# Two layers of windowed attention and experts on one core: layer 1 softmax shifts for two query blocks by one product, and the layer 0 output bias added on VectorE

## The chip, the cores and the metric

The kernel runs on one core of a Trainium2 chip. The metric is the device time of one execution in microseconds; lower is better. The engines are TensorE (PE; its weight loads are listed as PEld), VectorE (DVE), ScalarE (ACT), GpSimd (POOL) and SyncE (SP, which issues most of the DMAs). Every engine works through its own list of instructions in a fixed order, and semaphores make it wait for others.

## The reference, cut to what matters

The input x is 4 batches of 512 tokens with 128 features, in fp32. Two layers follow each other, and each is x + s * silu(f), where s is an attention and f a mixture of 8 experts, both on a normalised x.

```python
x = L0_attn_x
xn = _layernorm(x)
s = _L0_attn_ref(xn, ...)          # 16 heads of 8, keys of the last 64 tokens, scaled logits, then:
                                   #   out @ w_o + b_o
g = _silu(_L0_ffn_ref(xn, ...))    # one expert of 8 for each token: gelu(x @ w1 + b1) @ w2 + b2
x = x + s * g
xn = _layernorm(x)
s = _L1_attn_ref(xn, ...)          # layer norm, q, k, v, windowed attention, projection,
                                   #   then a dense gelu block of 512
g = _silu(_L1_ffn_ref(xn, ...))    # again one expert of 8 for each token, with relu
x = x + s * g
```

The windowed attention of layer 1 takes blocks of 64 queries with their own 64 keys, at steps of 32 tokens, and blends the overlapping halves:

```python
for i in range(0, S, w2):          # w2 = 32
    start, end = max(0, i - w4), min(S, i + window_size - w4)
    attn = softmax(einsum('bqd,bkd->bqk', qw, kw), axis=-1)
    wo = einsum('bqk,bkd->bqd', attn, vw)
    ...                            # blended with what the block before left
```

## The kernel before, in words

The kernel is one function, `two_layers`. Its work is written as 32 generators ("threads"), one for each stage: `project0`, `scores_q`, `fitness0`, `masked0`, `scores_k`, `values0`, `outs0` and `combine0` are the attention of layer 0; `prepare1`, `project1`, `queries1`, `scores_k1`, `values1`, `outs1`, `contexts1` and `feed1` that of layer 1; `route`, `moe_load`, `moe_load_2`, `moe_x`, `moe_h`, `moe_y` and `gates` the experts, once for each layer.

`run` (L357) interleaves the threads with a planner. Each step says what it needs, and after its instructions `spent(cost, steps, events)` books its cost on TensorE (times a pace of 1.12 after the first 70 us, and 1.8 before) and the steps that follow on the other engines. The planner takes the step that can start first, with the ranks listed at L1482 and after to break ties. The order on TensorE is the order in which steps are taken. Where the planner sees TensorE idle, `awake` (L113) puts in bf16 matmuls of ones into the bank that is about to be used, one for each 0.3 us of 0.8 times the gap. `copied` (L342) gives a copy out of PSUM to the engine, ScalarE or VectorE, that the books show free first.

The steps that the change touches:

- `outs0` (L1127). For each of the four batches it transposes the attention result into `attT`, and the output product `s` gets four groups of two fp32 matmuls: the bias row `o0` by a row of ones (1 row by 128), then `attT` by `wo0_sb`. If the gate of that batch is near, `combine` (L1160) multiplies straight from PSUM (L1163) and adds x (L1164); otherwise `copied` moves the sum to the tile `s0`, and `combine0` does that later. The new x is normalised in `prepare1` (L437 to L449 and `centred`, L428), which is what layer 1 and the router of the second expert pass start from.
- `queries1` (L1236). For each of 16 tiles (4 batches by 4 tiles of 128 tokens): products of scores `s1`, with queries on partitions, for two query blocks `w` of 64 in each of two parities `par`; their negated maxima `mx` (L1288); `split` (L465) writes each maximum as a sum of three bf16 terms into 12 of the 32 columns that a group of four heads has in `shb`; two bf16 transposes on TensorE (`tr_sh`) put these rows on partitions; ScalarE copies them to `shd` (L1296, 256 columns); four VectorE multiplications by `smask` (L1299) spread them over the four heads of a group into `sh4`.
- `scores_k1` (L1303). The products of scores again, now with keys on partitions (tile `e`): in each parity 8 fp32 matmuls of 32 rows by 64 columns, and then 8 bf16 matmuls that add the shifts, of 12 rows by 64 columns, since each query block needs its own columns of `sh4`. ScalarE takes the exponential of both halves (L1331). `values1` then multiplies by v.

The constants are made in a set-up that VectorE works through between the first layer norms: `jmask` (L840), `smask` (L842), `blend` (L826 to L828). L766 is the offset of a layer norm of layer 0, which ScalarE waits for. `feed1` (L1411) is layer 1's projection and dense block; its product `fy` for the last batch is the last on TensorE.

Of the kernel before, what the change touches and what calls it, by code (L numbers as in the profile page):

```python
# [16 lines left out]
P = 128  # L17
# [40 lines left out]
def two_layers(  # L58
# [145 lines left out]
    def prepared(name, n, shape, dtype=F32, one=None):  # L204
        got = []
        for i in range(n):
            t = const.tile(shape, dtype, tag=f"{name}{i}", name=f"{name}{i}")
            nc.gpsimd.memset(t, 0.0)
            if one:
                nc.gpsimd.memset(one(t), 1.0)  # L210
            got.append(t)
        return got
# [697 lines left out]
    for i in range(2):  # L910
        nc.gpsimd.tensor_copy(
            ves[i][:, 0 : H * VC].rearrange("p (h d) -> p h d", d=VC)[:, :, HD], valid[:, i : i + 1].to_broadcast([P, H])
        )
    shbs1 = prepared("shb1_", 2, [P, 2, G, 32], BF16)
    later.close()


# [209 lines left out]
    def outs0():  # L1127
        for i in range(NTILE):
            b, t = divmod(i, NT)
            yield "M", [("ov0", i)]  # L1130
            if t == 0:
                att0[b] = att_p.tile([P, NT, D], F32, tag="att0", name=f"att_{b}", bufs=1)
            tp = transposed(ovs0.pop(i), f"o0_{b}_{t}").rearrange("p (j g e) -> p j g e", j=J, g=G)
            rec = small.tile([P, J, G], F32, tag="rec0", name=f"rec0_{b}_{t}")
            nc.vector.reciprocal(rec, tp[:, :, :, HD])
            nc.vector.tensor_tensor(
                att0[b][:, t, :].rearrange("p (g j d) -> p j g d", g=G, j=J), tp[:, :, :, 0:HD],
                rec[:, :, :, None].to_broadcast([P, J, G, HD]), ALU.mult,
            )
            spent(0.5, [("D", 0.5)], [("o0", i)])  # L1140
            if t < NT - 1:
                continue
            yield "M", [("o0", i)]
            attT = tok.tile([P, T], F32, tag="attT", name=f"attT_{b}", bufs=1)
            copied(attT, transposed(att0[b], f"att_{b}"), 0.5, [("attT", b)])
            yield "M", [("attT", b)] + ([("x1", b - 1)] if b - 1 in s0 else [])
            ps = bank(f"s0_{b}")
            for u in range(NT):
                o = ps[:, u * D : (u + 1) * D]
                mm(o, ones[0:1, :], row("o0")[0:1], start=True, stop=False)  # L1150
                mm(o, attT[:, u * P : (u + 1) * P], wo0_sb, start=False, stop=True)
            ps = ps.rearrange("p (t d) -> p t d", t=NT)
            if at.get(("gate", 0, b), 1e9) < now["T"] + 3.0:
                combine(b, ps)
                spent(1.5, [("D", 0.7), ("D", 0.7)], [("so", b), ("x1", b), ("acc", 0, b)])
            else:
                s0[b] = tok.tile([P, NT, D], F32, tag="s0", name=f"s0_{b}", bufs=1)
                copied(s0[b], ps, 1.5, [("so", b)])

    def combine(b, s):  # L1160

# [40 lines left out]
    def project1():  # L1202

        for b in range(B):
            yield "-", [("xn1", b), ("s1", (b - 1) * NT - 1)]
            xh = tok.tile([P, NT, D], F32, tag="ln", name=f"xh_{b}", bufs=3)
            with behind_steps("A", at["xn1", b]):
# [28 lines left out]
    def queries1():  # L1236


        for i in range(NTILE):
# [49 lines left out]
                    mx.rearrange("p a g j -> p g a j")[:, 2 * gg : 2 * gg + 2], ps[gg], AX.X, ALU.max, negate=True,  # L1289
                )  # L1290
            shb = shbs1[i % 2]
            split(shb, mx, f"1_{b}_{t}")
            spent(1.15, [("D", 2.45), ("D", 1.0)], [("s1", i), ("shb", i)], scores=1)
            yield "M", [("shb", i), ("e1", i - 2)]
            shd = att_p.tile([P, 2 * P], BF16, tag="shd1", name=f"shd1_{b}_{t}")
            nc.scalar.copy(shd, transposed16(shb.rearrange("p a g r -> p a (g r)"), 2, f"sh1_{b}_{t}"))  # L1296
            sh4 = att_p.tile([P, 2, J, P], BF16, tag="sh4_1", name=f"sh4_1_{b}_{t}")
            for j in range(J):
                nc.vector.tensor_scalar_mul(sh4[:, :, j], shd.rearrange("p (a f) -> p a f", a=2), smask[:, j : j + 1])  # L1299
            asked1[i] = q4, sh4, v  # L1300
            spent(0.13, [("A", 0.4), ("D", 1.2)], [("sh1", i)])

    def scores_k1():  # L1303
        for i in range(NTILE):
# [9 lines left out]
            for par in range(2):  # L1314
                for w in range(2):
                    o = par * 2 * HALO + w * KB
                    for g in range(G):
                        r = slice(32 * g, 32 * g + 32)
                        mm(
                            ps[g // 2][w * KB : (w + 1) * KB, g % 2, par], kd[r, t * P + o : t * P + o + KB],  # L1320
                            q4[r, :, o : o + KB], start=True, stop=False,
                        )
                for w in range(2):
                    for g in range(G):
                        r = slice(32 * g, 32 * g + NS * J)
                        mm(
                            ps[g // 2][w * KB : (w + 1) * KB, g % 2, par], ones16[r, 0:KB],
                            sh4[r, par, :, w * KB : (w + 1) * KB], start=False, stop=True,
                        )
            for gg in range(2):  # L1330
                nc.scalar.activation(pt[:, 2 * gg : 2 * gg + 2], ps[gg], AF.Exp, scale=SCALE)  # L1331
            pts1[i] = pt, v
            spent(1.45, [("Ae", 1.03), ("Ae", 1.03)], [("e1", i)], scores=2)

    def values1():
        for i in range(NTILE):
# [223 lines left out]
```

## Time and profile before

| | |
|---|---|
| median of 3 runs | 489.83 us (489.01 to 495.69) |
| the profiled execution | 503.98 us |
| its span | 502.3 us |
| mean granted clock of TensorE | 0.941 |
| TensorE busy | 430.1 us, 86% |
| weight loads | 299.9 us, 60% |
| VectorE busy | 339.5 us, 68% |
| ScalarE busy | 261.2 us, 52% |
| GpSimd busy | 179.7 us, 36% |

A line of a group reads: line, engine, operation, the tile written and those read, the shapes, the number of records; then busy time in us and the mean of one record in ns; then the idle time ahead of them and what ended it. An fp32 matmul shows as two records. The line of a matmul or transpose is that of its helper (L83, L88), so they are told apart by tiles; the profile leaves out numbers in names, so that `s` is both the scores and the output sum, and `e` is the second product of scores in both layers. Records of matmuls overlap: their busy time is not the time that TensorE is held, which shows in the distance from one start to the next. A timeline line reads: start in us, time that the merged records cover in us, engine, line, operation, tiles, shapes, number of records, and idle time ahead in brackets. A windows line reads: stretch, its length, busy us (and records) of PE, PEld, DVE, ACT and POOL, the granted clock, the DMA share and GB/s.

### The profile page before, as it was taken

Reading aid. Unit: us, or ns where it says so; the run is one execution under the profiler, and the core shown is the slowest. Engines: PE = TensorE matmul, PEld = TensorE weight load, DVE = VectorE, ACT = ScalarE, POOL = GpSimd, SP = SyncE. Lnnn points to the kernel's source line nnn. Section 1 sums busy time; section 2 is a strip of 40 time slices with the busy share of each in tenths; the row PEclk is TensorE's granted clock in tenths of the full one; section 3 lists DMA queues with packets and bytes.
Section 4 is the critical chain, followed back from the end, with each engine's and each line's share of the span. In section 5 each row is a group of like instructions: output and inputs, shape, how many; then the busy total and the mean of one; then the engine's idle time right before and its main releaser. Section 6 shows DMA issues by size and latency. Waiting matters only on the chain.

```text
span 502.3 us, 14768 instructions
## 1 busy us (share of the span) xinstructions
PE 430.1 (86%) x5690; PEld 299.9 (60%) x5690; DVE 339.5 (68%) x1011; ACT 261.2 (52%) x512; POOL 179.7 (36%) x251
## 2 busy tenths in 40 slices
PE   5876887999999657799999899779889887899885
PEld 2642554676665432355565575557769676788763
DVE  6899987552855987887774658964556535765565
ACT  1422655696676644574436637445476333536522
POOL 5842444455422232342310304045342337532311
PEclk8787799999999996899999979999999998989999
DMA  5405444756253010100000000141452764532032
GB/s 168 129 1 140 120 139 117 220 135 181 43 129 97 16 54 23 42 23 2 18 8 3 1 1 23 35 126 29 124 169 65 170 167 124 163 96 68 18 103 65
DMA packets 61894, 42.12 MB, mean 84 GB/s; under 512 B 11328, under 2 KB 54208, under 8 KB 61824
## 3 DMA queue, kind: packets, MB, share of 16 engines
q1 hardware_dynamic: 58464, 34.85, 25.3%
q0 software_dynamic: 2944, 6.04, 4.4%
q8 instruction: 45, 0.74, 0.6%
q10 hardware_dynamic: 416, 0.29, 0.2%
q14 instruction: 25, 0.20, 0.1%
HBM read 34.99 MB, written 6.16 MB: 82 GB/s over the span
## 4 chain that ended last, share of the span: by engine, by line
PE 57%; DVE 25%; issue 8%; ACT 7%; POOL 2%; DMA 1%; SPq 0%; DVEq 0%; ACTq 0%; POOLq 0%
PE e L83 11%; PE s L83 8%; PE h L83 7%; PE y L83 6%; PE ov L83 5%; DVE mx L1009 3%; PE fy L83 3%; PE f L83 2%; ACT th L1017 2%; DVE mx L1288 2%; PE pr L83 2%; PE v L83 2%; PE qkv L83 1%; PE o L88 1%; DVE sm L1009 1%
## 5 line engine op out<-in xcount | busy, mean ns | idle before, releaser
L666 POOL DMA_INDIRECT yt<-yb,put_at x46 | 46.2, 1005 | 105.3 <-DVE yb L664 21.0
L609 POOL DMA_INDIRECT xb<-xd,tokens_at x46 | 45.3, 985 | 56.6 <-DVE tokens_at L586 16.9
L83 PE MATMUL h<-xbT,wb 128*128 128x128 f32 x368 | 51.4, 290 | 3.0 <-ACT xbT L344 1.3
L83 PE MATMUL y<-wb,hb 128*128 128x128 f32 x368 | 49.3, 282 | 3.3 <-ACT hb L696 2.5
L83 PEld LDWEIGHTS h<-xbT,wb 128*128 128x128 f32 x368 | 46.3, 201 | 9.7 <-issue 4.1
L83 PE MATMUL e<-q,kd 32*64 32x256 f32 (+1 forms) x864 | 48.4, 444 | 1.5 <-issue 0.9
L83 PEld LDWEIGHTS y<-wb,hb 128*128 128x128 f32 x368 | 45.3, 195 | 7.1 <-ACT hb L696 2.9
L1288 DVE TENSOR_REDUCE mx<-s 128x16 f32<-128x1024 f32 x32 | 37.6, 1218 | 7.8 <-PE s L83 5.9
L1331 ACT ACTIVATE pt<-e 128x1024 f32<-128x1024 f32 x32 | 31.0, 1021 | 20.5 <-PE e L83 17.4
L1017 ACT ACTIVATE th<-s 128x768 f32<-128x768 f32 x32 | 26.0, 814 | 29.8 <-DVE mx L1009 29.2
L83 PE MATMUL s<-k,qd 32*32 32x384 f32 (+1 forms) x1024 | 37.4, 473 | 2.6 <-ACT pt L1331 2.3
L83 PEld LDWEIGHTS <-ones 12*64 12x64 bf16 (+2 forms) x434 | 21.4, 107 | 26.5 <-issue 18.6
L344 ACT COPY osb<-ov 128x512 f32<-128x512 f32 x32 | 18.1, 587 | 35.1 <-PE ov L83 26.4
L1106 ACT ACTIVATE pt<-e 128x1024 f32<-128x1024 f32 x32 | 31.0, 1021 | 10.1 <-PE e L83 10.1
L1009 DVE TENSOR_REDUCE mx<-s 128x8 f32<-128x768 f32 x32 | 29.3, 950 | 8.0 <-PE s L83 6.6
L696 ACT ACTIVATE hb<-h,bb 128x128 f32<-128x128 f32 x92 | 26.6, 381 | 14.3 <-PE h L83 10.8
L83 PE MATMUL ov<-pt,va 64*32 64x128 f32 (+1 forms) x896 | 30.6, 290 | 3.2 <-issue 2.8
L1009 DVE TENSOR_REDUCE sm<-th 128x8 f32<-128x768 f32 x32 | 30.1, 946 | 1.1 <-ACT th L1017 0.7
L1249 POOL TENSOR_TENSOR q<-qd,jmask 128x640 f32<-128x640 f32 x16 | 19.9, 1257 | 29.6 <-PE e L83 27.4
L83 PEld LDWEIGHTS e<-q,kd 32*64 32x64 f32 x864 | 20.6, 136 | 14.6 <-issue 9.7
L344 DVE COPY osb<-ov 128x512 f32<-128x512 f32 x16 | 11.0, 688 | 23.8 <-PE ov L83 17.1
L83 PEld LDWEIGHTS ov<-pt,va 64*32 64x32 f32 (+1 forms) x896 | 17.6, 106 | 10.7 <-issue 6.0
(287 smaller groups left out, 922.4 us busy)
## 6 DMA issues: line engine op xcount, KB each, us to landing
wb<-in_w SPq DMA_DIRECT2D x92, 256.0 KB
bb<-in_b SPq DMA_DIRECT2D x46, 64.0 KB
acc<-yt SPq DMA_DIRECT2D x8, 256.0 KB
xd<-ln_a SPq DMA_DIRECT2D x4, 256.0 KB
xd<-xr SPq DMA_DIRECT2D x4, 256.0 KB
out<-acc SPq DMA_DIRECT2D x8, 128.0 KB
x<-in_x SPq DMA_DIRECT2D x3, 256.0 KB
bb<-in_cols SPq DMA_DIRECT2D x46, 2.0 KB
```

The lines of the kernel that those rows point to most:

```text
L83: ins = nc.tensor.matmul(*args, **kw)
L88: ins = nc.tensor.transpose(dst, src, ident)
L344: (nc.scalar.copy if e == "A" else nc.vector.tensor_copy)(dst, src)
L609: nc.gpsimd.indirect_dma_start(out=xb, out_offset=None, in_=xd, in_offset=bass.IndirectOffsetOnAxis(ap=tokens_at[:, k : k + 1], axis=0),)
L666: nc.gpsimd.indirect_dma_start(out=yt, out_offset=bass.IndirectOffsetOnAxis(ap=routed[n][0][:, k : k + 1], axis=0), in_=y, in_offset=None,)
L696: nc.scalar.activation(h[:, c, :], src[:, c * P : (c + 1) * P], AF.Gelu, bias=bias[:, c : c + 1])
L1009: nc.vector.tensor_reduce(dst[:, t, 8 * gg : 8 * gg + 8].rearrange("p (u j) -> p u j", u=2), src.rearrange("p u (j f) -> p u j f", j=J), A ...
L1017: nc.scalar.activation(th, ps[gg], AF.Tanh, scale=0.5 * SCALE)
L1106: nc.scalar.activation(pt[:, 2 * gg : 2 * gg + 2], ps[gg], AF.Exp)
L1249: engine.tensor_tensor(dst, src[:, None, o : o + TW].to_broadcast([P, J, TW]), jmask[:, :, None].to_broadcast([P, J, TW]), ALU.mult,)
L1288: nc.vector.tensor_reduce(mx.rearrange("p a g j -> p g a j")[:, 2 * gg : 2 * gg + 2], ps[gg], AX.X, ALU.max, negate=True,)
L1331: nc.scalar.activation(pt[:, 2 * gg : 2 * gg + 2], ps[gg], AF.Exp, scale=SCALE)
```

## The change

Two edits, and their set-up.

1. Layer 0: the matmul of the bias row is gone from the output sums. VectorE adds the row `o0` as it reads the bank: into a tile `s0` of its own ahead of `combine`, or in place of the copy. The cost booked for the step goes from 1.5 to 1.1.
2. Layer 1: `split` writes into a tile `terms`; one more VectorE operation writes `shb` with each query block's 12 terms in the block's own half of the group's 32 columns, by a multiplication with `own` (1 for the rows of that block, else 0). The transposes become two products by `fold` (two 64x64 identities, one above the other), so that `shd` has 64 columns a parity instead of 128, and 24 of a group's 32 rows are used. `sh4` halves likewise, with `smask1`. In `scores_k1` one bf16 matmul of 32 rows by 128 columns (`lane`) for each group replaces two of 12 rows by 64 columns. Booked costs: 0.13 to 0.1 on TensorE for the products, 1.45 to 1.25 for `scores_k1`, 1.0 to 1.25 on VectorE for the split, 1.2 to 0.9 for `sh4`.
3. `own`, `fold`, `lane` and `smask1` are made by six VectorE operations, written at the start of `project1`.

```diff
+    own = const.tile([P, 2], BF16, tag="own", name="own")
+    fold = const.tile([P, KB], BF16, tag="fold", name="fold")
+    lane = const.tile([P, P], BF16, tag="lane", name="lane")
+    smask1 = const.tile([P, J], F32, tag="smask1", name="smask1")
...
-                mm(o, ones[0:1, :], row("o0")[0:1], start=True, stop=False)
-                mm(o, attT[:, u * P : (u + 1) * P], wo0_sb, start=False, stop=True)
+                mm(o, attT[:, u * P : (u + 1) * P], wo0_sb, start=True, stop=True)
             ps = ps.rearrange("p (t d) -> p t d", t=NT)
             if at.get(("gate", 0, b), 1e9) < now["T"] + 3.0:
-                combine(b, ps)
-                spent(1.5, [("D", 0.7), ("D", 0.7)], [("so", b), ("x1", b), ("acc", 0, b)])
+                s = tok.tile([P, NT, D], F32, tag="s0", name=f"s0_{b}", bufs=1)
+                nc.vector.tensor_tensor(s, ps, row("o0")[:, None, :].to_broadcast([P, NT, D]), ALU.add)
+                combine(b, s)
+                spent(1.1, [("D", 0.7), ("D", 0.7), ("D", 0.7)], [("so", b), ("x1", b), ("acc", 0, b)])
             else:
                 s0[b] = tok.tile([P, NT, D], F32, tag="s0", name=f"s0_{b}", bufs=1)
-                copied(s0[b], ps, 1.5, [("so", b)])
+                nc.vector.tensor_tensor(s0[b], ps, row("o0")[:, None, :].to_broadcast([P, NT, D]), ALU.add)
+                spent(1.1, [("D", 0.7)], [("so", b)])
...
+            if b == 0:
+                yield "-", [("mask", 0)]
+                half = small.tile([P, 2, 2], F32, tag="half", name="half", bufs=1)
+                nc.vector.tensor_reduce(half[:, 0], ident.rearrange("p (w q) -> p w q", w=2), AX.X, ALU.add)
+                nc.vector.tensor_copy(own, half[:, 0])
+                nc.vector.tensor_tensor(fold, ident16[:, 0:KB], ident16[:, KB:P], ALU.add)
+                nc.vector.tensor_reduce(
+                    smask1, ident.rearrange("p (g s j) -> p j g s", g=2 * G, j=J)[:, :, :, 0:NS], AX.XY, ALU.add
+                )
+                nc.vector.tensor_reduce(half[:, 1], ident.rearrange("p (g c r) -> p c g r", g=G, c=2), AX.XY, ALU.add)
+                nc.vector.tensor_copy(lane.rearrange("p (c k) -> p c k", c=2), half[:, 1, :, None].to_broadcast([P, 2, KB]))
+                spent(0, [("D", 1.3)], [("lane", 0)])
...
-            split(shb, mx, f"1_{b}_{t}")
-            spent(1.15, [("D", 2.45), ("D", 1.0)], [("s1", i), ("shb", i)], scores=1)
+            terms = small.tile([P, 2, G, NS * J], BF16, tag="terms", name=f"terms_{b}_{t}", bufs=1)
+            split(terms, mx, f"1_{b}_{t}")
+            nc.vector.tensor_tensor(
+                shb.rearrange("p a g (c r) -> p (a g) c r", c=2)[:, :, :, 0 : NS * J],
+                terms.rearrange("p a g r -> p (a g) r")[:, :, None].to_broadcast([P, 2 * G, 2, NS * J]),
+                own[:, None, :, None].to_broadcast([P, 2 * G, 2, NS * J]), ALU.mult,
+            )
+            spent(1.15, [("D", 2.45), ("D", 1.25)], [("s1", i), ("shb", i)], scores=1)
             yield "M", [("shb", i), ("e1", i - 2)]
-            shd = att_p.tile([P, 2 * P], BF16, tag="shd1", name=f"shd1_{b}_{t}")
-            nc.scalar.copy(shd, transposed16(shb.rearrange("p a g r -> p a (g r)"), 2, f"sh1_{b}_{t}"))
-            sh4 = att_p.tile([P, 2, J, P], BF16, tag="sh4_1", name=f"sh4_1_{b}_{t}")
+            shd = att_p.tile([P, 2, KB], BF16, tag="shd1", name=f"shd1_{b}_{t}")
+            ps = bank(f"sh1_{b}_{t}")[:, 0 : 2 * KB].rearrange("p (a f) -> p a f", a=2)
+            for par in range(2):
+                mm(ps[:, par], shb[:, par].rearrange("p g r -> p (g r)"), fold, start=True, stop=True)
+            nc.scalar.copy(shd, ps)
+
+            sh4 = att_p.tile([P, 2, J, KB], BF16, tag="sh4_1", name=f"sh4_1_{b}_{t}")
             for j in range(J):
-                nc.vector.tensor_scalar_mul(sh4[:, :, j], shd.rearrange("p (a f) -> p a f", a=2), smask[:, j : j + 1])
+                nc.vector.tensor_scalar_mul(sh4[:, :, j], shd, smask1[:, j : j + 1])
             asked1[i] = q4, sh4, v
-            spent(0.13, [("A", 0.4), ("D", 1.2)], [("sh1", i)])
+            spent(0.1, [("A", 0.33), ("D", 0.9)], [("sh1", i)])
...
-                for w in range(2):
-                    for g in range(G):
-                        r = slice(32 * g, 32 * g + NS * J)
-                        mm(
-                            ps[g // 2][w * KB : (w + 1) * KB, g % 2, par], ones16[r, 0:KB],
-                            sh4[r, par, :, w * KB : (w + 1) * KB], start=False, stop=True,
-                        )
+                for g in range(G):
+                    r = slice(32 * g, 32 * g + 32)
+                    mm(ps[g // 2][:, g % 2, par], lane[r], sh4[r, par], start=False, stop=True)
...
-            spent(1.45, [("Ae", 1.03), ("Ae", 1.03)], [("e1", i)], scores=2)
+            spent(1.25, [("Ae", 1.03), ("Ae", 1.03)], [("e1", i)], scores=2)
```

## The prediction

> **What bounds the kernel now.** I read the span and busy rows first, then the chain that ended last, then the stages by windows, then single stretches of the timeline.
>
> ```profile
> span 502.3 us, 14768 instructions
> ...
> PE 430.1 (86%) x5690; PEld 299.9 (60%) x5690; DVE 339.5 (68%) x1011; ACT 261.2 (52%) x512; POOL 179.7 (36%) x251
> ...
> PE 57%; DVE 25%; issue 8%; ACT 7%; POOL 2%; DMA 1%; SPq 0%; DVEq 0%; ACTq 0%; POOLq 0%
> ```
>
> TensorE carries more than half of the chain and VectorE a quarter, so microseconds saved on TensorE count in some stages and in others do not. The windows (us of each engine in a stretch: PE, PEld, DVE, ACT, POOL) tell which.
>
> ```profile
> 127.00:147.00 20.00, 20.00 (x251) 13.03 (x250) 12.85 (x38) 14.08 (x24) 7.82 (x9) 1.00 0.31 68
> 147.00:250.00 103.00, 84.77 (x1130) 50.10 (x1134) 81.84 (x203) 57.51 (x104) 30.54 (x31) 0.93 0.13 37
> 250.00:300.00 50.00, 47.34 (x794) 30.69 (x795) 30.01 (x85) 24.50 (x45) 6.99 (x9) 0.96 0.03 7
> 300.00:338.00 38.00, 30.49 (x531) 21.70 (x530) 30.25 (x126) 20.49 (x36) 11.82 (x14) 0.95 0.22 61
> 338.00:465.00 127.00, 114.79 (x1704) 94.83 (x1705) 72.30 (x212) 63.28 (x151) 52.22 (x56) 0.96 0.42 116
> ```
>
> TensorE is full in 127 to 147, 250 to 300 and 338 to 465. From 147 to 250 VectorE is as busy as TensorE, and from 300 to 338 the routing of the second expert pass runs on VectorE while TensorE has 7.5 us idle.
>
> **Layer 0 sums (outs0).** The timeline shows one of the four output products:
>
> ```profile
> 130.62 0.48 PE L83 MATMUL s<-rowb,ones 1*128 1x128 f32 x2
> 131.03 0.49 PE L83 MATMUL s<-wo_sb,attT 128*128 128x128 f32 x2
> 131.45 0.48 PE L83 MATMUL s<-rowb,ones 1*128 1x128 f32 x2
> ...
> 133.94 0.43 PE L83 MATMUL e<-bands_k,diag 32*32 32x512 bf16 x16
> ```
>
> Bias and product alternate, each takes 0.415 us, and eight take 3.32 us (130.62 to 133.94). Without the bias four full products stay. The nearest row for four of them in a row is the expert product y, eight records (two for each fp32 matmul), in the chain:
>
> ```profile
> 108.80 0.89 PE y L83 x8
> ```
>
> So 3.32 becomes 0.89: 2.43 us less TensorE for each of four batches. For the third (237.5) the first real product started at 237.95 because attT was just landing, so 2.05 remain. The whole is 3 x 2.43 + 2.05 = 9.3 us. The addition costs VectorE one 128x512 operation a batch; the neighbour L1163 with the same shapes takes 0.69 us. For batch 0 it replaces ScalarE's copy of 0.59; for the other three it stands ahead of L1163 and L1164.
>
> What of it reaches the end:
> - Batch 0 (130.6) and batch 3 (293.4) lie where TensorE is full: -2.4 each. After batch 3 TensorE goes on with other tiles while the sum is added, so the addition is covered there; without that cover it costs 0.7.
> - Batch 1 (197.3): TensorE would be done at 198.3, but VectorE is on L428 and L448/L449 until 200.23. Then three operations of 0.69 replace two that began at 200.80. Saved 0.57, paid 0.69: +0.1.
> - Batch 2: TensorE done at 238.8, VectorE free at 239.35 after L1299; three operations end at 241.45 instead of 242.38: -0.9.
>
> Sum: -5.6 us, against 9.3 on TensorE alone.
>
> **Layer 1 shifts (scores_k1).** This is the disputed part. The matmul count halves (256 to 128), and the row of the by-form groups looks like a prize:
>
> ```profile
> L83 PE MATMUL e<-sh,ones 12*64 12x256 bf16 x256 | 15.0, 290 | 1.6 <-issue 1.6
> L83 PE MATMUL e<-sh,ones 12*128 12x512 bf16 x64 | 6.5, 398 | 0.0
> ```
>
> Half of 15.0 would be 7.5 us. But these are overlapping records. The timeline of one tile says what a shift costs:
>
> ```profile
> 383.58 0.69 PE L83 MATMUL e<-q,kd 32*64 32x256 f32 x16
> 384.07 0.32 PE L83 MATMUL e<-sh,ones 12*64 12x256 bf16 x8
> 384.18 0.75 PE L83 MATMUL e<-q,kd 32*64 32x256 f32 x16
> 384.61 0.43 PE L83 MATMUL e<-sh,ones 12*64 12x256 bf16 x8
> 384.97 0.33 PE L88 MATMUL xt<-ident,xb 128*128 128x128 f32 x1
> ```
>
> All eight run at once on eight array tiles of 32x64 and hold TensorE for 0.11 us (384.07 to 384.18); scores and shifts follow each other without a gap, since both use that tile shape. The new matmuls are 32x128: four at once, the same 256 columns, again 0.11 us. Nothing is saved. But the shape now changes between scores and shifts. Layer 0 shows the price of that:
>
> ```profile
> 141.50 0.39 PE L83 MATMUL e<-sh,ones 12*128 12x512 bf16 x4
> 141.82 0.44 PE L88 MATMUL tr_o<-ident,osb 128*128 128x128 f32 x2
> ```
>
> Four shifts of 512 columns need 2 x 0.107 = 0.21; the next shape begins 0.32 after them: 0.11 us lost. The scores ahead of them have their last start at 141.17 and need 0.21; the shifts start at 141.50: 0.11 again. A new tile has three more changes than an old one (scores to shifts, back, and again), 0.34 us: 1.39 (383.58 to 384.97) becomes 1.73, and 16 tiles make +5.4 us. Bounds: 0 if the drain is hidden, 0.20 a change (the bias pairs above lose about that: 0.415 less 0.22), so 0 to +9.6; 0.11 is the same pair of shapes. Nearly all tiles lie where TensorE is full; I count 14 of 16: **+4.7 us**.
>
> Here two statements of the Trainium skill pull apart, both on the page "TensorEngine Tiling (Array Packing)". Its section "Instruction Overhead" puts about 60 cycles on each matmul; at the 2.4 GHz of the page "TensorE: Matmul & The Clock Gate", 25 ns, 128 fewer matmuls would give an estimate of -3.2 us. Its "Key Properties" say that a change of tiling mode drains the engine, which speaks against this change and gives no figure. The trace sides with the second: eight shifts start 7 ns apart ((0.32 - 0.27) / 7), so a count brings nothing, and the drain is 0.11. By the first rule the part is -3.2, by the row +5.4.
>
> **The rest of a layer 1 tile.** VectorE gains the product by own: 192 elements. L1380 (32 elements) takes 0.19, L1163 (512) 0.69; on that line 0.35. [...] I take 0.35. The four L1299 halve to 128 elements: today four take 0.88; L560, same size and type, repeats every 0.16, so four take about 0.74: -0.15. ScalarE's copy goes from 0.376 to about 0.28 (its xbT copy of 128x128). The two transposes become products of 64 columns: 0 to -0.05. So VectorE gets +0.2 a tile, 3.2 us in all, and the chain from scores to shifted queries stays within 0.1. VectorE is a quarter of the path: +0.8.
>
> **Set-up.** The order of instructions puts six new operations (three reductions, a fold and two copies) on VectorE right ahead of L766, the offset of the first normalisation. VectorE has no gap there (8.1 to 14 us), ScalarE's first normalisation waits for L766, and everything follows it. Neighbours of that size repeat every 0.15 to 0.2 us: **+1.1 us**, all on the path. Range 0.6 to 1.5.
>
> **The moved order.** The planner is given other costs, and its order changes. Up to the fourth batch's layer norm the order on TensorE is the same; from there the second expert pass and layer 1's tiles are interleaved anew. Its first expert product now stands behind tr_hn_1_0, the kd/qd products and f_1_0; VectorE's tokens_at stands behind rec/att of another tile (some 1.2 us), so POOL's gathers start later; SP's weight loads of the second pass move too, each behind its value loads. Between the fourth sum and the first experts the planner puts 17 idle-filling matmuls where it had 5 (136 in all against 114, 0.216 us each). It books a score tile at 1.25 x 1.12 = 1.40, where I expect 1.73, so part of the idle time that it sees will not be there. Fillers in a real gap cost nothing (20 of them ahead of tokens_0 ended 1.4 us before their data). Filler and order: between -4 and +8; I take +1.
>
> **Sum.** -5.6 + 4.7 + 0.8 + 1.1 + 1 = +2.0 on the profiled execution, 503.98 (span 502.3 and 1.7 around it), so 506.0. That execution is slower than the median of the runs, 489.83; scaled by 0.972 it is +1.9: **491.7 us**, no change by the 2% that a measurement of this kernel can tell.
>
> **Rivals.**
> - **Idle in front of the second expert pass (slower).** Place: 293 to 345. For: the 17 planned fillers stand for 17 x 0.3 / 0.8 = 6.4 us of idle, 5 stood for 1.9; VectorE is at 95% from 310 to 330 and cannot deliver sooner. If TensorE stands for these 4.5 and the experts pushed behind cannot be packed later (another 3.5, four expert products), it is 8 above my sum: 514 there, 499.5 in the runs. It decides once TensorE is idle for over 15 us from 300 to 345, twice the present. Against: distances between producers and users in the new order are about as long as before. 0.20.
> - **No drain, and the count pays (faster).** -9.3 - 7.5 + 0.8 + 1.1 = -15: 475 in the runs. Only the busy sums speak for it; the timeline does not. 0.06.
> - **The sums count in full, the rest as I have it.** -9.3 + 7.6 = -1.7: 488. Against it: VectorE at 147 to 250. In the same class, 0.22.
> - **It doesn't do what it says:** were the planner to put the sums apart instead of fusing, the additions would move; the order shows three batches fused, as before.
>
> **How the numbers follow.** My forecast 0.52, sums in full 0.22, idle 0.20, no drain 0.06. The range must reach towards both ends: 483 to 503. Half of the idle rival stays under 2%, but large drains (0.20 a change, +4) could take others over it: faster 0.06, same 0.74, slower 0.20.
>
> **What would show it.** A score tile of layer 1 at about 1.7 us with 0.1 gaps around the shifts; four output products in 0.9 to 1.0 us; L766 about 1 us later; VectorE's busy time up by some 6 to 7 us. Wrong: a score tile still at 1.4, or the end of fy_3_2 moved by over 8 us.

## The result, and the profile after

On one chip the changed kernel took 510.96 us in the median of 4 runs, the kernel before 492.23: a ratio of 1.036, with a 95% interval of 1.029 to 1.043. It is slower, and outside the forecast range (491.7, 483 to 503). Chips differ (the kernel before takes 494 us on one and 508 on another), so below only ratios to the kernel before within one series are compared; the ratios leave out the runs that were disturbed. Most ratios below differ from 1 by less than 2%, so read the intervals behind them (95%) and not the ratios alone.

The page of the changed kernel:

```profile
span 507.5 us, 14524 instructions
...
PE 417.2 (82%) x5552; PEld 287.6 (57%) x5552; DVE 340.5 (67%) x1035; ACT 260.2 (51%) x513; POOL 179.9 (35%) x251
...
PE 8%; DVE 3%; ACT 1%; issue 1%; POOL 1%; DMA 1%; SPq 0%; DVEq 0%; POOLq 0%; ACTq 0%
```

TensorE is 12.9 us less busy than before and the kernel is slower: work left, and waits came. The chain's shares are small because it could be followed back only to 424 us, to a scatter that landed then. That will matter. The same windows as before:

```profile
127.00:147.00 20.00, 17.25 (x268) 11.49 (x267) 15.20 (x32) 11.62 (x20) 8.64 (x10) 1.00 0.42 94
147.00:250.00 103.00, 81.51 (x1152) 48.02 (x1140) 82.15 (x210) 56.53 (x102) 29.33 (x31) 0.92 0.12 34
250.00:300.00 50.00, 43.14 (x733) 26.46 (x731) 32.45 (x98) 27.16 (x48) 8.43 (x12) 1.00 0.01 2
300.00:338.00 38.00, 32.96 (x458) 22.37 (x459) 28.09 (x111) 21.28 (x39) 11.82 (x12) 0.96 0.29 78
338.00:465.00 127.00, 108.92 (x1648) 87.27 (x1646) 69.69 (x227) 57.25 (x141) 50.54 (x56) 0.93 0.41 109
```

The three stretches in which TensorE was full (127 to 147, 250 to 300, 338 to 465) now hold 2.8, 6.9 and 18.1 us of idle time, against 0.0, 2.7 and 12.2 before.

Three things that the prediction named can be read at once. In the timeline of TensorE, the four output products alone:

```profile
126.16 1.16 PE L83 MATMUL s<-wo_sb,attT 128*128 128x128 f32 x8
127.24 0.43 PE L83 MATMUL e<-bands_k,diag 32*32 32x512 bf16 x16
```

1.08 us from start to start, where 0.9 to 1.0 was forecast and 3.32 stood. A score tile of layer 1:

```profile
391.70 0.69 PE L83 MATMUL e<-q,kd 32*64 32x256 f32 x16
392.32 0.29 PE L83 MATMUL e<-sh,lane 32*128 32x256 bf16 x4
392.54 0.69 PE L83 MATMUL e<-q,kd 32*64 32x256 f32 x16
393.16 0.29 PE L83 MATMUL e<-sh,lane 32*128 32x256 bf16 x4
393.38 0.33 PE L88 MATMUL xt<-ident,xb 128*128 128x128 f32 x1
```

From 391.70 to 393.38 it is 1.68 us; 1.73 was forecast and 1.39 stood. And on VectorE the offset that ScalarE waits for:

```profile
10.70 0.23 DVE L1222 CAST lane<-half 128x128 bf16<-128x128 f32 x1
10.84 0.15 DVE L766 SCALAR_TENSOR_TENSOR off<-mv,rs 128x4 f32<-128x4 f32 x1
```

It starts 0.9 us later than before, behind the last set-up operation; 1.1 was forecast. In the kernel before it stood here:

```profile
9.92 0.16 DVE L766 SCALAR_TENSOR_TENSOR off<-mv,rs 128x4 f32<-128x4 f32 x1
```

So these three behave about as priced. What the kernel makes of these prices is another matter.

The two profiled executions are 5.2 us apart (502.3 and 507.5), the medians 18.7: the one of before (503.98 us) was slower than its own median. A second profile of the changed kernel, on a chip where before takes 505.94 us, stands better beside it: a span of 519.7 us. I use that one to find the time. The two are still executions on two chips, so a difference of a few us in one stretch can be theirs and not the change's.

### The profile page after: what moved, and what is told of

Its sections match the earlier page's. It is cut to its first block, busy times and chain, and to the rows that moved or that the text cites. A ratio compares the mean times of both kernels' runs of the same rounds, so it can differ in the third digit from the quotient of the medians.

```text
span 507.5 us, 14524 instructions
## 1 busy us (share of the span) xinstructions
PE 417.2 (82%) x5552; PEld 287.6 (57%) x5552; DVE 340.5 (67%) x1035; ACT 260.2 (51%) x513; POOL 179.9 (35%) x251
## 5 line engine op out<-in xcount | busy, mean ns | idle before, releaser
L83 PE MATMUL y<-wb,hb 128*128 128x128 f32 x368 | 50.4, 285 | 3.1 <-ACT hb L696 1.6
L83 PE MATMUL e<-q,kd 32*64 32x256 f32 (+1 forms) x864 | 44.4, 454 | 0.4 <-ACT pt L1111 0.4
L83 PE MATMUL s<-k,qd 32*32 32x384 f32 (+1 forms) x1024 | 35.3, 462 | 3.3 <-ACT pt L1356 2.7
L696 ACT ACTIVATE hb<-h,bb 128x128 f32<-128x128 f32 x92 | 26.4, 381 | 12.0 <-PE h L83 10.9
L83 PE MATMUL ov<-pt,va 64*32 64x128 f32 (+1 forms) x896 | 29.2, 299 | 0.4 <-ACT pt L1356 0.3
L83 PEld LDWEIGHTS <-ones 128*128 128x128 bf16 (+1 forms) x200 | 15.1, 101 | 23.7 <-issue 14.1
L704 ACT ACTIVATE hb<-h,bb 128x128 f32<-128x128 f32 x56 | 15.8, 374 | 19.3 <-PE h L83 19.3
L88 PE MATMUL o<-ident,osb 128*128 128x128 f32 x128 | 18.1, 285 | 9.1 <-DVE osb L344 8.9
L664 DVE TENSOR_TENSOR yb<-y,bb 128x128 f32<-128x128 f32 x46 | 12.7, 283 | 18.6 <-PE y L83 17.5
```

Source lines behind the costliest of these rows:

```text
L83: ins = nc.tensor.matmul(*args, **kw)
L88: ins = nc.tensor.transpose(dst, src, ident)
L696: nc.scalar.activation(h[:, c, :], src[:, c * P : (c + 1) * P], AF.Gelu, bias=bias[:, c : c + 1])
```

## The experiments

### Four kernels that take the change apart

First theory: the sum of the instructions is right and the moved order is not. Two switches, instructions and order, make a square. The order on TensorE follows the booked costs alone, so it can be set without the instructions.

`a_old_books`: all instructions of the change, booked as before. On TensorE its steps stand in the order of before.

```diff
-    spent(1.25, [("Ae", 1.03), ("Ae", 1.03)], [("e1", i)], scores=2)
+    spent(1.45, [("Ae", 1.03), ("Ae", 1.03)], [("e1", i)], scores=2)
...
```

> The changed kernel's instructions with the costs booked as before the change, so that TensorE works through its steps in the order of before (116 fillers against 114). If the moved order is to blame for the loss: within 1% of before (488 to 497 us), since the sum of the instructions alone was +1 us. If the new instructions are to blame (array-shape changes, VectorE work): as slow as the changed kernel, 507 us or more.

Measured: 1.0117 (1.0029 to 1.0206), 511.9 against 507.61 us: just over the 1% expected of the first theory, and far under the second.

`b_new_books`: the instructions of before, booked as in the change. Its order on TensorE is that of the changed kernel. What the planner decides by its books goes with it: the order on the other engines, 14 more idle-filling matmuls than before, two more copies of osb on ScalarE (34 instead of 32), and the first batch's sum is copied by VectorE.

```diff
-    spent(1.45, [("Ae", 1.03), ("Ae", 1.03)], [("e1", i)], scores=2)
+    spent(1.25, [("Ae", 1.03), ("Ae", 1.03)], [("e1", i)], scores=2)
...
```

> The instructions of before with the costs booked as in the change, so that TensorE works through its steps in the order of after (128 fillers against 136). If the moved order is to blame: 505 to 515 us, with the last expert product y behind the projection pr of the last batch and the end set by the gates' loads of yt and their tanh. If the instructions are to blame: 490 to 495 us.

Measured: 1.0262 (1.0193 to 1.0331). **The order alone, with none of the change's new instructions in it, costs 2.6%**, and 1.0117 x 1.0262 is 1.038, where the whole change has 1.036.

`layer0_only` and `layer1_only`: one part of the change each, in the order of before.

> Only the bias edit of layer 0, with the order of before. The prediction's sum for this part: -5.6 us, so about 487 us (1.1% faster); if the added VectorE work takes it back, 492; if all of TensorE's 9.3 us count, 483.

> Only the layer 1 edit with its set-up, with the order of before. The prediction's sum: +4.7 for shape changes, +0.8 VectorE, +1.1 set-up = +6.6 us, so about 499 us (1.3% slower), and a score tile of 1.68 us. If the drain doesn't count on the path: 494.

Measured: 0.9969 (0.9935 to 1.0003), where 1.1% less was expected, and 1.0146 (1.0071 to 1.022), as expected. Their product, 1.0115, is what both give together. In us of this series' 507.61: layer 0 -1.6, layer 1 +7.4, order +13.3.

### Where the order's time lies

I cut each profile at four of its own events: the start of the first product by wo_sb in the first output sum, that in the fourth, VectorE's `tokens_at` (the routing of the second expert pass is known), the end of the last fy, and the end. These are the windows of before, the end of the last fy being 497.97 (columns as before: PE, PEld, DVE, ACT, POOL, clock, DMA share, GB/s):

```profile
131.03:293.78 162.75, 141.87 (x2071) 87.23 (x2070) 117.88 (x304) 91.83 (x165) 42.63 (x46) 0.96 0.13 33
293.78:330.59 36.81, 31.28 (x531) 22.51 (x530) 28.76 (x113) 17.80 (x29) 6.97 (x8) 0.91 0.15 38
330.59:497.97 167.38, 149.33 (x2052) 120.66 (x2052) 96.25 (x297) 80.51 (x182) 65.48 (x72) 0.97 0.39 107
497.97:502.28 4.31, 0.00 (x1) 0.00 (x0) 1.27 (x3) 0.00 (x0) 0.00 (x0) 0.84 0.10 30
```

The last two of `b_new_books`, the same instructions in the new order:

```profile
330.29:509.31 179.02, 150.97 (x2055) 120.75 (x2053) 86.62 (x283) 80.04 (x181) 66.66 (x72) 0.94 0.35 96
509.31:517.28 7.97, 0.00 (x1) 0.00 (x0) 4.58 (x11) 0.74 (x2) 0.00 (x0) 0.78 0.25 74
```

And the four of the changed kernel's second profile:

```profile
133.41:298.00 164.59, 136.96 (x2018) 83.26 (x2017) 120.25 (x311) 92.06 (x165) 42.93 (x47) 0.95 0.12 33
298.00:335.29 37.29, 31.10 (x507) 20.32 (x506) 32.15 (x123) 17.54 (x29) 7.05 (x8) 0.91 0.18 47
335.29:510.58 175.29, 153.17 (x1991) 118.09 (x1988) 89.38 (x291) 78.61 (x181) 66.14 (x72) 0.97 0.36 95
510.58:519.73 9.15, 0.00 (x0) 0.00 (x0) 4.58 (x11) 1.26 (x2) 0.00 (x0) 0.67 0.38 106
```

Up to the routing `b_new_books` is where before is (330.29 against 330.59). After it the stretch is 11.6 us longer, and TensorE idle in it for 28.1 us (179.02 less 150.97) instead of 18.1. The tail grows from 4.3 to 8.0. Idle 10.0 and tail 3.7 make 13.7 of the 15.0 us between the two spans; by the medians the order costs 13.3. The tail is sure: it is 4.3 or 4.4 us in every trace of the old order. The idle time is less so: in the traces of `layer0_last` and `layer0_only`, both in the old order, it is 16.7 and 21.5 us, and in the changed kernel's two 22.9 and 22.1, so 4 to 5 more than before and not 10.

The tail has one reading. After the last fy before had three operations of VectorE and a store left. The chain of waits of the changed kernel (start, us, what) ends otherwise:

```profile
500.30 0.91 PE pr L83 x8
...
508.72 2.95 DMA acc<-yt
...
511.75 0.64 ACT tg L682
...
512.41 0.70 DVE acc L683
```

`gates` cannot start before the last scatter of expert outputs, and that hangs on `y_1_22`, which the new order puts behind fy and pr; before it stood ahead of them. With two `acc` buffers the last two batches' gates follow the first two, so one late product carries four gates after it.

For the idle time the first profile of the changed kernel has a striking place, in the timeline of POOL, VectorE and TensorE:

```profile
423.74 1.01 POOL L666 DMA_INDIRECT yt<-yb,put_at  x1 [0.30 <-issue]
426.97 0.98 POOL L666 DMA_INDIRECT yt<-yb,put_at  x1 [2.22 <-issue]
427.98 1.26 POOL L1268 TENSOR_TENSOR q<-qd,jmask 128x640 f32<-128x640 f32 x1
429.40 1.00 POOL L609 DMA_INDIRECT xb<-xd,tokens_at  x1 [0.16 <-issue]
430.43 0.73 POOL L393 TENSOR_TENSOR rs_d<-rs_d,neghalf 128x2 f32<-128x2 f32 x1
431.19 0.60 DVE L428 TENSOR_SCALAR hn<-xr,mv_d,rs_d 128x128 f32<-128x128 f32 x2 [9.00 <-POOL rs_d L393]
431.71 0.68 DVE L344 COPY osb<-ov 128x512 f32<-128x512 f32 x1
...
432.54 1.94 PE L88 MATMUL o<-ident,osb 128*128 128x128 f32 x8 [8.89 <-DVE osb L344]
```

Read it upwards. TensorE is idle 8.89 us for the copy of osb; the copy stands on VectorE behind `hn`; `hn` waits 9.00 us for a power of two columns on GpSimd; and GpSimd's queue holds a scatter that starts 2.22 us after the one before it has ended (the profile names no releaser there; that it waited for that one to land is my reading), then a product, then a gather. Everything on that list is cheap. A 10.2 us spell at half the granted clock begins inside the wait, at 427.3. The next four kernels test whether this, or the late output, is the order's price.

### The power and the late output

`after_again` is the changed kernel once more. `after_no_pow` and `before_no_pow` leave GpSimd's power out of feed1, in either order. `after_y70` changes one rank.

```diff
-                rsqrt(rs, mv[:, :, 1], LN_EPS)
+                nc.vector.tensor_scalar_add(rs, mv[:, :, 1], LN_EPS)
...
-        (moe_y(1, yt1), 121, 71, 113, 127),
+        (moe_y(1, yt1), 121, 71, 113, 70),
```

> The changed kernel once more, to stand beside the next three on one chip. The two halves of the change, run before, put it at the product of the instructions alone in the old order (1.012) and the new order alone (1.026): 1.038 of the kernel before; the first measurement gave 1.036. Expected 1.03 to 1.045, and in its trace again a stretch near 424 to 432 us where TensorE is idle for over 5 us ahead of the transposes of osb.

> The changed kernel in the same order on TensorE, without GpSimd's power of -1/2 in feed1's eight layer norms: VectorE goes on with the variance plus epsilon itself (this part of the computation is left out). Theory 1, GpSimd's queue: the new order puts one power behind a gather, two scatters of expert outputs of which the second waits for the first to land, and a product; VectorE waits 9.0 us for it with the copy of osb behind it, TensorE 8.9, and a half-clock spell of 10 us follows, which costs up to 5 more. Then this kernel is 9 to 14 us faster than the changed one, 1.010 to 1.020 of before. Theory 2, the late last expert output: the end hangs on the last scatter and the gates, so the gain is under 4 us, 1.030 or more. Theory 3, the new order is worse all along, a little at each place: 3 to 5 us, 1.028.

> The same part left out of the kernel before, in its own order. There the eight waits of VectorE for GpSimd's power come to 8.1 us in all, and TensorE's idle time in front of the transposes of hn behind them to 2.4. Theory 1: 2 to 4 us faster, 0.992 to 0.996, far less than the same edit gives in the new order. If it gains as much as there (9 us or more, 0.982), the power costs in every order and the new order is not to blame by it.

> The changed kernel with the rank of the last batch's expert output products set from 127 to 70, so that the planner takes y_18 to y_22 of the second pass before fy and pr of the third batch instead of behind them; nothing else in the order changes ahead of the last 60 us. Theory 2 (late last output): the last output moves from 475.7 back to about 468, the gates' tanh with it, and the run gets 5 to 8 us faster, 1.022. Theory 1: the end of TensorE's work stays where the 8.9 us of idle have put it, so 0 to 3 us, 1.030 to 1.036.

Measured: 1.0381 (1.0261 to 1.05), 1.026 (1.0171 to 1.035), 0.987 (0.9775 to 0.9965) and 1.0352 (1.0258 to 1.0446). In the second profile of the changed kernel the striking place is gone by itself: TensorE waits 0.8 us there instead of 8.9, and it has its idle time elsewhere. So `after_again` met its time and missed its trace. **My theory of GpSimd's queue fell**: without the power the new order gains 1.2% and the old one 1.3%. The power costs some 6 us in either, with intervals of about 1% on each ratio, and nothing shows that the new order makes it dearer. The late output fell too, as a cause of its own. The rank put the tail right:

```profile
338.02:519.26 181.24, 157.29 (x1997) 121.17 (x1994) 90.20 (x292) 81.63 (x190) 65.96 (x72) 0.94 0.37 98
519.26:523.61 4.35, 0.00 (x1) 0.00 (x0) 1.27 (x3) 0.00 (x0) 0.00 (x0) 0.97 0.11 30
```

4.35 us instead of 9.15, and the stretch ahead of it is 6 longer; the median stayed (525.39 and 525.07 us). That suggested two chains of nearly equal length.

`after_y70_no_pow` has both edits.

> Both repairs of the new order at once: the last batch's expert outputs earlier, and feed1's power left out (VectorE goes on with the variance plus epsilon). Alone they gave 0.3% and 1.2%. Theory 1, two chains of nearly the same length end together (TensorE's last products, and the last scatter with the gates): each repair alone is stopped by the other, both together give about 10 us, ratio 1.015 to 1.020. Theory 2, the new order costs TensorE's stretch everywhere and the tail is no limit of its own: the sum of the two, 5 to 6 us, ratio 1.023 to 1.027.

Measured: 1.0145 (1.0085 to 1.0204), 2.4 points under the changed kernel, where the single edits gave 0.3 and 1.2. It fits the two chains; the intervals are too wide to exclude a plain sum. And it does not clear the order: the old order with the power left out (0.987) times the instructions (1.0117) is 0.9985, so about 1.6% of the order's 2.6% is still there, with intervals of 0.6 to 1.0 points on the ratios it is made of.

`after_ex0` lets the planner bring the experts forward in the new order:

```diff
-        (moe_x(1), 67, 40, 46, 72),
+        (moe_x(1), 2, 40, 46, 72),
...
-        (moe_y(1, yt1), 121, 71, 113, 127),
+        (moe_y(1, yt1), 4, 71, 113, 70),
...
-        (moe_h(1, relu), 60, 3, 122, 105),
+        (moe_h(1, relu), 3, 3, 122, 105),
```

> The changed kernel with other ranks for the second pass's experts (first batch's x, h, y products at ranks 2, 3, 4, the last batch's y at 70), so that the first expert products stand ahead of kd, qd and f_1_0, as in the order of before, and the last y ahead of fy of the third batch. Theory A, the new order costs because it pushes the experts back at the start and the gates wait for the last: first output at 360 to 368 us after the start instead of 376, the tail behind the last fy 4.3 instead of 9.2, ratio 1.012 to 1.022. Theory B, every order that the planner finds from these booked costs leaves TensorE the same idle time: 1.030 to 1.040, and the 21 more filler matmuls show where.

Measured: 1.0468 (1.0421 to 1.0516), the slowest of all. Its first output comes at 356 us and its tail is 4.4, as theory A wanted, yet TensorE is idle for 25.6 us between `tokens_at` and the last fy. Bringing the experts forward does not repair the order, though other steps moved with them. Theory B, that any order from these books leaves the idle time, is nearer, but its 1.030 to 1.040 was too low, and 25.6 is more than the 22 of the changed kernel, in spite of 61 filler matmuls in that stretch against 40.

### Layer 0: which batch counts

`layer0_no_add` leaves the bias out altogether, `layer0_last` changes the last batch alone. Both are in the order of before.

```diff
-                mm(o, ones[0:1, :], row("o0")[0:1], start=True, stop=False)
-                mm(o, attT[:, u * P : (u + 1) * P], wo0_sb, start=False, stop=True)
+                if b < B - 1:
+                    mm(o, ones[0:1, :], row("o0")[0:1], start=True, stop=False)
+                mm(o, attT[:, u * P : (u + 1) * P], wo0_sb, start=b == B - 1, stop=True)
```

> The kernel before without the bias of layer 0's output sums altogether (the bias is left out): four products a batch on TensorE, no addition on VectorE. Theory 1, the stretch from the first to the fourth sum is set by VectorE and what follows it: TensorE's 7 us of saved time there turn into idle time (idle 27 to 29 us instead of 21, its length 161 to 163 as before), and only the fourth batch's 2.5 us are gained: 0.990 to 0.996. Rival, TensorE is full at the first sum and the additions took the gain away: the stretch gets 4 to 6 us shorter and the ratio falls to 0.985 or less.

> The change of layer 0 for the last batch alone, the first three as before, in the order of before. Theory 1: the last batch is the only one whose 2.4 us count, and the other three cost VectorE 0.7 each in a stretch that it bounds, so this is as good as all four or better: 0.993 to 0.997 (all four: 0.997). Rival: each batch is worth the same, a quarter of the gain of all four, 0.999.

Measured: 0.9949 (0.9916 to 0.9981) and 0.9947 (0.9915 to 0.9978). One batch changed is as good as four by these intervals, and as good as no bias at all. The windows of `layer0_only` (all four batches) say why, for the first two stretches:

```profile
132.11:300.15 168.04, 142.48 (x2047) 89.81 (x2046) 118.32 (x307) 91.96 (x164) 43.52 (x47) 0.91 0.12 32
300.15:334.39 34.24, 27.24 (x521) 20.17 (x520) 30.57 (x116) 17.80 (x29) 7.30 (x8) 0.95 0.15 41
```

From the first to the fourth sum TensorE is idle for 25.6 us instead of 20.9, and in the changed kernel for 27.6. Most of the 7 us saved there came back as idle time. (Its length of 168.0 also holds a lower granted clock, 0.91 against 0.96, so I read only the idle time from it.) This holds in all traces of this case: 18.6 to 21.7 us of idle where the first three batches keep their bias products, 25.3 to 28.6 where they don't. VectorE's three additional operations are not the reason, since `layer0_no_add` has none of them and 25.3 us (27 to 29 were expected). From the fourth on, the stretch falls from 36.8 to 34.2 us, and in `layer0_last` it is 34.4. That looks like the last batch's saving, but the stretch is as short in `layer1_again`, which keeps all bias products (and 37.1 in `layer1_only`, the same kernel):

```profile
293.46:328.08 34.62, 29.44 (x507) 20.00 (x506) 28.91 (x116) 17.37 (x29) 6.98 (x8) 1.00 0.14 35
```

So that the last batch's saving is the one that stays rests on the ratio of `layer0_last`, not on this stretch. `layer0_last` is the version to keep: **0.5% faster than the kernel before**, and the only kernel here that computes the whole reference with an interval under 1.

### Layer 1: what its 7 us are

`layer1_narrow` cuts each shift product into two of 64 columns, on the tile shape of the scores.

```diff
-                    mm(ps[g // 2][:, g % 2, par], lane[r], sh4[r, par], start=False, stop=True)
+                    for w in range(2):
+                        c = slice(w * KB, (w + 1) * KB)
+                        mm(ps[g // 2][c, g % 2, par], lane[r, c], sh4[r, par], start=False, stop=True)
```

> Layer 1's part alone, in the order of before, but each shift product cut into its two halves of 64 columns: 256 products of 32 rows by 64 columns on the tile shape of the scores, all else as in layer 1's part. Theory 1, the change of shape costs: the score tile falls from 1.68 back to 1.39 us, 14 of 16 tiles give 4 us, and the ratio falls from 1.015 to 1.005 to 1.008. Rival, the cost is VectorE's new product and the set-up: the ratio stays at 1.012 to 1.018 and the doubled count may even add to it.

It has no ratio (median of all runs 515.41 against 509.0 us), so I took it again beside layer 1's part, with a kernel that has all repairs so far.

> Layer 1's part alone once more, on one chip with the next. Theory 1 (change of tile shape): 1.010 to 1.020 of before, score tile 1.68 us.

> Layer 1's part with the shift products in halves of 64 columns, once more, since its first comparison stayed open. Theory 1: the changes of shape cost 4 us, so 1.003 to 1.010, under layer 1's part in the same call by 0.6 to 1.0%. Rival (VectorE's new product and the set-up are the cost): within 0.3% of layer 1's part.

> The order of before, layer 0's change for the last batch only, and layer 1's part with the shift products in halves: the change with the three costs found so far taken out. Theory 1: 0.995 from layer 0 times 1.005 from layer 1, 0.997 to 1.004. If it stays above 1.008, layer 1's set-up and VectorE's product weigh more than the 2 us that I gave them.

Measured: 1.0143 (1.0101 to 1.0185), 1.0137 (1.0068 to 1.0206) and 1.0115 (1.005 to 1.018). `repaired` missed its 0.997 to 1.004 as well: it agrees with what its two halves gave, 0.9947 x 1.0137 = 1.008. The score tile of `layer1_narrow_again` did what was asked of it, in the timeline of TensorE:

```profile
365.56 0.69 PE L83 MATMUL e<-q,kd 32*64 32x256 f32 x16
366.05 0.32 PE L83 MATMUL e<-sh,lane 32*64 32x256 bf16 x8
366.16 0.76 PE L83 MATMUL e<-q,kd 32*64 32x256 f32 x16
366.59 0.43 PE L83 MATMUL e<-sh,lane 32*64 32x256 bf16 x8
366.95 0.33 PE L88 MATMUL xt<-ident,xb 128*128 128x128 f32 x1
```

1.39 us again, with twice the products: the price of a change of shape, 0.10 us ((1.68 - 1.39) / 3), is real. The time did not follow: 0.06 points less, where 0.8 were expected. The interval of 0.7 points on either side does not settle it, but the rival had the better of it, and I tested its two halves.

`layer1_late` issues the six set-up operations behind the first sum; `layer1_no_own` leaves out VectorE's product by own.

```diff
+                with behind_steps("D", at["so", 0]):
...
-            split(terms, mx, f"1_{b}_{t}")
-            nc.vector.tensor_tensor(
...
+            split(shb, mx, f"1_{b}_{t}")
```

> Layer 1's part alone, with its six set-up operations issued on VectorE behind the first layer 0 sum (about 130 us) instead of ahead of L766. If the set-up costs its 1.1 us at the start and no more, L766 is back at 9.9 us and the ratio falls from 1.014 to 1.012. If everything that follows a late start is moved against the clock's windows and pays more, it falls to 1.008 or less. If the start doesn't count at all, 1.014.

> Layer 1's part alone without VectorE's product by own (the terms of both query blocks stay in the first 12 of a group's columns; the masking is left out). If VectorE's 16 products of 0.35 us and the wait they add between scores and shifted scores are the cost of layer 1's part, 3 to 5 us go: ratio 1.003 to 1.008. If it is the changes of tile shape, of which the halves of 64 columns showed no gain, the ratio stays at 1.012 to 1.016.

Measured: 1.0162 (1.0083 to 1.0242) and 1.007 (1.0033 to 1.0107). With the set-up moved L766 is back in its old place, and nothing is gained that can be seen:

```profile
9.94 0.16 DVE L766 SCALAR_TENSOR_TENSOR off<-mv,rs 128x4 f32<-128x4 f32 x1
```

The product by own is about half of layer 1's cost: without it 1.007 remain of 1.0143, and in the same series `layer1_late`, which keeps it, has a median of 500.89 us against 497.25. I looked for the way it gets to TensorE in the idle time (behind the last bar, us) ahead of the transposes or products that take shb; first in layer 1's part (`layer1_again`), then without the product, then in the kernel before, which never had it:

```profile
L83 PE MATMUL sh<-fold,shb 128*128 128x64 bf16 x32 | 3.7, 197 | 6.5 <-DVE shb L1311 6.5
```

```profile
L83 PE MATMUL sh<-fold,shb 128*128 128x64 bf16 x32 | 3.7, 199 | 3.2 <-DVE shb L472 3.1
```

```profile
L88 PE MATMUL tr_sh<-ident,shb 128*128 128x128 bf16 x48 | 6.3, 228 | 6.7 <-DVE shb L472 6.2 <-DVE osb L344 0.2
```

From the first to the second, 3.3 us of waiting go, and 0.7% of the time (3.6 us of 494.5). The product (16 of 0.354 us, 5.7 us of VectorE) does stand in the chain from scores to shifted scores. But the kernel before waits for shb about as long without it (6.2 us), and 5.6 us in `layer1_only`, the same kernel as `layer1_again`. So the time that the product costs is shown, and the way it takes to TensorE is not. The other half of layer 1's cost stays open.

## Why the prediction was wrong, step by step

**The moved order** is the step that failed. I saw that the order changed, and where: the later first expert product, `tokens_at` behind another tile, more fillers. I priced it at +1 (range -4 to +8), and held against the slow rival that "distances between producers and users in the new order are about as long as before". The instructions of before in that order cost +13.3 us. What showed in place of it: the distance from `which` to `tokens_at` went from 8.6 to 10.8 us (I had written 1.2 more, it is 2.2), `y_1_22` went behind fy and pr, which opened a second chain to the end and made the tail 3.7 to 4.8 us longer, and TensorE was idle for 4 to 10 us more in the stretch ahead of it. The place of the last output was not priced at all. Of the order's 2.6%, the late output and GpSimd's power together account for about 1.0; the rest is idle time in changing places that no single edit removed, and its cause stays open.

**The rival of the slow side** had a fifth of the chances and a wrong place. TensorE's idle time from 300 to 338 fell from 7.5 to 5.0 us; its mark, over 15 us from 300 to 345, was not reached (5.6 us). The idle time came after 338.

**Layer 0** was priced at -5.6 and gave -1.6. Its last batch behaved: alone it has 0.9947, 2.7 us of 509.0, and -2.4 was forecast. The first three were booked at -3.2 together and gave nothing that can be seen (all four have 0.9969). The largest term of them is batch 0: I read that TensorE is full from 127 to 147 and booked -2.4, but from 147 to 250 VectorE is as busy as TensorE, and a TensorE that is early there waits. No run changed batch 0 alone, so that it is this term is inferred.

**Layer 1** was priced at +6.6 with the set-up (4.7 + 0.8 + 1.1) and gave +7.4. The total is right by luck, since its parts are not. The rows were read well (1.68 us a tile, 0.10 for a change of shape, L766 0.9 later), but the two that I put on the path, drains and set-up, showed no gain in time when they were taken away (their intervals would hide a part of it), and VectorE's work, given +0.8 since "VectorE is a quarter of the path", is worth about 3.5 with its product alone. I had argued that the chain from scores to shifted queries stays within 0.1 us. The estimate of -3.2 us from the Trainium skill's 60 cycles for each matmul ("TensorEngine Tiling (Array Packing)", "Instruction Overhead") fails here once more: a tile with sixteen shift products on the scores' shape takes 1.39 us, one with eight on another shape 1.68. Products that run side by side on tiles of the array do not add up so.

**VectorE's busy time** rose by 1.0 us, not 6 to 7: the planner gave ScalarE two more of the osb copies (34 instead of 32), and the multiplications into sh4 fell from 16.5 to 12.2 us in all, not to 14. These two make 3.3 of the 5 to 6 us; the rest I did not follow.

**The sum** of +2.0 holds +1.0 for the changed instructions, which cost +5.9 in the old order. That miss of 5 us the range covered. The order's 13.3 it did not cover.

## What to carry to other kernels

When a planner writes the order, a changed cost in its books is a change of its own: run the old instructions under the new books, and the new ones under the old, before pricing anything else. A saving on the bounding engine counts only until the next stretch with another bound, so ask of each microsecond which wait it meets next. And a small operation on an engine that is not the fullest can cost a good part of its time if it stands between two steps of the full one: here 3.6 of 5.7 us.

## What the runs showed of the hardware

A change of the array's tile shape between 32x64 and 32x128 costs 0.10 us (1.68 us for a score tile with three more changes, 1.39 without), near the 0.11 that the prediction read from a neighbouring pair of shapes. Shift products of 32 rows cost no more than those of 12: the tile takes 1.39 us with either.

In the changed kernel's first trace the granted clock is one half in spells of 3.41, 6.83 and 10.24 us, which are one, two and three times the shortest (the last spell is cut off by the end). One of them begins at 427.3 us, 3.7 us into the wait of 8.89, and lasts to 437.5, 5 us beyond the wait's end.

I had not expected how far two executions of one kernel, here on two chips, differ: the same TensorE order lost 8.9 us in one place in one execution and 0.8 in the next, at about the same total idle time (22.9 and 22.1 us between `tokens_at` and the last fy).
